# A selective-scan layer with an interleaved feed-forward network: evicting the mask and delta products from PSUM with one copy

## Chip, cores and metric

The kernel runs on one core of a Trainium2 chip. Its time is the device time in microseconds (us) of one execution. The profile is of one further execution, taken with the hardware profiler.

## What is computed

The input is x, two sequences of 1024 tokens with 512 features, 2048 tokens in all. A selective state-space layer and a feed-forward network follow each other, each with a residual and a layer norm:

```
xn    = x * rsqrt(mean(x*x) + 1e-6) * norm_w
mask  = sigmoid((xn @ select_proj_w.T + select_proj_b) * select_gate)
xn    = xn * mask
delta, B, C = split(xn @ x_proj_w.T)          # 128 columns each
delta = softplus(delta @ dt_proj_w.T + dt_proj_b)
h_t   = exp(delta_t * A) * h_{t-1} + (delta_t * xn_t) * B_t   # A = -exp(A_log), state 512 x 128
y_t   = h_t . C_t
x     = layernorm(x + (y + x * D) @ out_proj_w.T)
x     = layernorm(x + (silu(x @ w_gate.T) * (x @ w_up.T)) @ w_down.T)   # hidden 2048
```

All arithmetic is fp32. The change touches the two nonlinear stages ahead of the scan. The mask is a sigmoid and delta a softplus. The kernel makes both from softplus(v) = relu(v) + log(1 + exp(-|v|)). The sigmoid of z is exp(-softplus(-z)). So each stage needs the ReLU and the absolute value of the same product, taken with factors that differ from feature to feature (a bias, and for the mask a scale as well).

## The kernel before

The scan sets the frame. A main loop makes 1024 steps, k = 0 to 1023. Sixteen steps make a segment of 32 tokens (`st`), and eight make one half of the features of a segment. In a step:

- TensorE (PE) makes two matmul pairs that are interleaved: `bu` (L689), the input of step k, and `a` (L407), the decay of step k+1.
- ScalarE (ACT) turns the two halves of `a` into exp(-a) in SBUF (L414, the exps). They are written one step ahead of the scan that uses them, in a buffer of three steps. `a` has two PSUM banks.
- VectorE (DVE) adds the carried state to the first column (L708) and scans 32 tokens (L709).
- GpSimd (POOL) builds the operands `ddt` (L378) and `du` (L388) of coming steps.
- In some steps PE makes the outputs `y` of the half before (L426).

All other work is written as Python generators, and `work`, a small planner, mixes it in while the program is built. Nothing is decided on the chip: each engine runs its instructions in the order in which they were written. A generator yields "P" where it wants TensorE, "H" between pieces of matmul work that it holds TensorE for, and "E" where other engines must do something first. In the steps where the list `PARTS` gives a credit (4, 0, 3, 3, 0, 3, 3, 0 over eight steps), `work.give_back()` runs first and lets the generator that has just used TensorE go on: its eviction from PSUM then stands on ACT ahead of the exps of that step. After the exps `work.others()` lets every generator that stands at "E" go one yield further. After the scan, `work.tensor()` gives out pieces of matmul work up to the credit. All of this work shares one PSUM bank in the main loop (the tile "m" of `misc`, one buffer): the next piece of matmuls must wait until ACT or DVE has read the last one. During the start, before the loop, there are six such banks.

The generators are `pre(c)`, which prepares one lot of tokens for the scan; `post(tt)`, the output projection and first layer norm of 128 tokens; `ffn(tt)`, their feed-forward network; and `silu`, the activation of one piece of it. There are nine lots: two of 128 tokens (four segments each), then seven of 256 (eight segments each).

`pre(c)` runs through these stages, each needing the one before: squares and their sum (`ss`); the factor `rms`; the mask product `sel` in four pieces m, each evicted by L221 (ReLU into `u`) and L225 (absolute value into `dt`); `softplus` (Exp L318, Ln L320, two additions on POOL L323); an Exp (L230); the product with xn on POOL (L233); the products `xp` and `b`; the delta product `z` in two pieces of two features blocks, evicted by L273 and L274 for each block; `softplus` again; the product `u` on POOL (L278); its transposes `uT`, one for each 128 tokens (copy L290, then four DMAs L295 to DRAM `ub_d`); and `t`, the first delta of each segment (copy L313, DMA L314). The tiles into which L290 and L313 copy are one buffer, the tile "row": each copy waits until the DMAs that read the one before have landed.

`pre(0)` runs by itself before the loop. `pre(c+1)` is put in front of the planner's list when lot c begins. If it is not finished one segment before its tokens are due, `work.finish` writes all that is left of it at once, between two steps, together with what the other generators have at "E":

```
if lot_of[st + 1] > c:
    work.finish(pres[c + 1])
load(st + 1)
```

For lot 2 that point lies between step 111 and step 112.

Of the kernel before, what the change touches and what calls it, by code (L numbers as in the profile page):

```python
# [10 lines left out]
AF = mybir.ActivationFunctionType  # L11
# [14 lines left out]
V_NORM, V_SELB, V_GATE, V_DTB = range(4)  # L26
# [8 lines left out]
def kernel(  # L35
# [17 lines left out]
    nc = tc.nc  # L53
# [8 lines left out]
    NM = D // P  # L62
# [40 lines left out]
    gate_b = main.tile([P, NM], FP, name="gate_b")  # L103
    neg = main.tile([P, 2, NM], FP, name="neg")
# [37 lines left out]
    def col(group, m):  # L142
        return vec[:, group, m : m + 1]
# [13 lines left out]
    def misc(name):  # L157
        return bank_pool[0].tile([P, 512], FP, tag="m", name=name)
# [5 lines left out]
    def pre(c):  # L164

        t0, n = lots[c]
# [8 lines left out]
        dt = pre_pool.tile([P, NM, TC], FP, tag="dt", name=f"dt_{c}", bufs=2)  # L175
        u = pre_pool.tile([P, NM, TC], FP, tag="u", name=f"u_{c}")
        c_sb = pre_pool.tile([P, TC], FP, tag="c_sb", name=f"c_sb_{c}", bufs=2)
        rms, low, c_sb = rms[:, 0:n], low[:, 0:n], c_sb[:, 0:n]
        xT, dt, u = xT[:, :, 0:n], dt[:, :, 0:n], u[:, :, 0:n]
# [3 lines left out]
        def matmuls(ps, w, m, rhs):  # L183
            for k in range(NM):
                nc.tensor.matmul(  # L185
                    ps[:, 0:n], w[:, k, ts(m, P)], rhs[:, k, :],
                    start=(k == 0), stop=(k == NM - 1),
                )
                yield "H" if k + 1 < NM else "E"
# [10 lines left out]
        ps = misc(f"ss_{c}")  # L200
# [14 lines left out]
        yield "P"  # L215


        for m in range(NM):
            ps = misc(f"sel_{c}_{m}")
            yield from matmuls(ps, sel_w, m, xn)  # L220
            nc.scalar.activation(  # L221
                u[:, m, :], ps[:, 0:n], AF.Relu,
                bias=neg[:, 1, m : m + 1], scale=neg[:, 0, m : m + 1],
            )
            nc.scalar.activation(  # L225
                dt[:, m, :], ps[:, 0:n], AF.Abs, bias=gate_b[:, m : m + 1], scale=col(V_GATE, m)
            )
            yield "P" if m + 1 < NM else "E"
        yield from softplus(dt, u)
        nc.scalar.activation(dt, dt, AF.Exp, scale=-1.0)  # L230
        yield "E"
# [8 lines left out]
        for g, dst in ((0, low), (2, c_sb)):  # L240
            ps = misc(f"xp_{c}_{g}")
# [4 lines left out]
        ps = misc(f"b_{c}")  # L246
# [17 lines left out]
        for a in range(0, NM, 2):  # L264
            ps = misc(f"z_{c}_{a}")
            for m in (a, a + 1):
                nc.tensor.matmul(  # L267
                    ps[:, ts(m - a, n)], dt_w[:, ts(m, P)], low, start=True, stop=True
                )
                yield "H" if m == a else "E"  # L270
            for m in (a, a + 1):
                z = ps[:, ts(m - a, n)]
                nc.scalar.activation(u[:, m, :], z, AF.Relu, bias=col(V_DTB, m))  # L273
                nc.scalar.activation(dt[:, m, :], z, AF.Abs, bias=col(V_DTB, m))  # L274
            yield "P" if a == 0 else "E"
        yield from softplus(dt, u)
        for a in (slice(0, 2), slice(2, 4)):
            nc.gpsimd.tensor_tensor(u[:, a, :], dt[:, a, :], xn[:, a, :], ALU.mult)  # L278
# [2 lines left out]
        for j in range(n_j):  # L281
            yield "P"
            ps = misc(f"uT_{c}_{j}")
# [5 lines left out]
            t = pre_pool.tile([P, D], FP, tag="row", name=f"uT_{c}_{j}")  # L289
# [14 lines left out]
        ps = misc(f"t0_{c}")  # L304
# [7 lines left out]
        t = pre_pool.tile([P, D], FP, tag="row", name=f"t0_{c}")  # L312
# [3 lines left out]
    def softplus(a, r):  # L316

        nc.scalar.activation(a, a, AF.Exp, scale=-1.0)  # L318
        yield "E"
        nc.scalar.activation(a, a, AF.Ln, bias=ones[:, 0:1])  # L320
        yield "E"
        for m in (slice(0, 2), slice(2, 4)):
            nc.gpsimd.tensor_tensor(a[:, m, :], a[:, m, :], r[:, m, :], ALU.add)  # L323
            yield "E"
# [72 lines left out]
    def place(k):  # L397
        h, r = divmod(k, 8)
        m, pair = divmod(r, 2)
        return h, m, pair  # L400
# [247 lines left out]
    work = Work()  # L648

    def run(gen):  # L650
        for _ in gen:
            pass

    run(pre(0))
    diag(0, 2)
    diag(0, 3)
# [9 lines left out]
    for k in range(NG):  # L666
        h, m, pair = place(k)
# [5 lines left out]
        if r == 0:  # L673
            hs[h] = half_pool.tile([P, 256, S], FP, tag="h", name=f"h_{h}")
            if i == 0:
                c = lot_of[st]
                if c + 1 < NC and c not in begun:
                    begun.add(c)
                    pres[c + 1] = work.add(pre(c + 1), front=True)
                if st + 1 < NS:  # L680
# [3 lines that stand above are left out]
# [135 lines left out]
```

## Time and profile before

| What | Value |
|---|---|
| Median of 3 runs | 2833.24 us (2833.19 to 2833.54) |
| Profiled execution, its own time | 2842.96 us |
| Profiled execution, span from first to last instruction | 2841.2 us |
| PE busy | 2727.4 us (96%) |
| DVE busy | 2522.9 us (89%) |
| ACT busy | 1549.8 us (55%) |
| POOL busy | 1783.3 us (63%) |
| First scan begins | 43.22 us |
| Last scan ends | 2760.64 us |

The times in a profile are microseconds from the start of the span. In the timeline, each row has its start, its length, the engine, the source line, the operation, output and input, and in brackets the idle time ahead of it with what ended it. PEld are weight loads of TensorE, which run beside its matmuls; PE is busy by a model of where a matmul ends, so its 96% is not a peak rate. An fp32 matmul shows as two records. In the groups by form, the figures are the total busy time, the mean duration in ns, and the idle time ahead with the engine that ended it.

### The profile page before, as it was taken

The page shows a single profiled execution, that of the slowest core. Times are in us where ns is not written, and L with a number is a line of the kernel's source. Part 1 is how long each engine was busy: PE and PEld are TensorE (multiplying, and loading weights), DVE is VectorE, ACT ScalarE, POOL GpSimd, SP SyncE. Part 2 cuts the span into 40 slices and gives each one's busy share as a digit, 9 for nine tenths or more (in the row PEclk, how much of TensorE's full clock was granted, in tenths as well). Part 3 has the DMA queues.
Part 4 walks back from the last instruction along what each step waited for, and adds up shares of the span by engine and source line. Part 5 has one row for each costly group of instructions (what it writes and reads, how often), then busy time and mean ns, then how long its engine had stood idle before and what let it go on. Part 6 is the DMA issues. An engine that isn't in the chain of part 4 may idle for free.

```text
span 2841.2 us, 57463 instructions
## 1 busy us (share of the span) xinstructions
PE 2727.4 (96%) x22728; PEld 1484.1 (52%) x22728; DVE 2522.9 (89%) x2144; ACT 1549.8 (55%) x3105; POOL 1783.3 (63%) x2016
## 2 busy tenths in 40 slices
PE   7879999999999999999999999999999999999998
PEld 4324554555555554555544555555555555555558
DVE  2999898999999999999999999999999999999980
ACT  4546555555565455654656556555555554555442
POOL 4556675666667675775667667667576666657552
PEclk7999999999999999999999999999999999999999
DMA  2012222224223232233312333132331323332336
GB/s 75 16 30 66 86 77 79 87 73 134 86 62 116 86 121 64 83 96 105 123 43 84 105 104 104 57 100 93 112 101 47 113 87 109 101 105 96 107 103 208
DMA packets 112380, 258.67 MB, mean 91 GB/s; under 512 B 11568, under 2 KB 49456, under 8 KB 112112
## 3 DMA queue, kind: packets, MB, share of 16 engines
q1 hardware_dynamic: 112112, 254.99, 27.6%
q8 instruction: 181, 2.97, 0.4%
q14 instruction: 87, 0.71, 0.1%
HBM read 242.23 MB, written 12.71 MB: 90 GB/s over the span
## 4 chain that ended last, share of the span: by engine, by line
PE 75%; DVE 18%; issue 3%; ACT 2%; POOL 1%; DMA 0%; SPq 0%; DVEq 0%; POOLq 0%; ACTq 0%
PE bu L689 28%; PE gu L532 17%; DVE h L709 15%; PE y L426 13%; PE d L552 7%; PE a L407 4%; PE sel L185 2%; PE op L473 1%; PE xp L185 1%; DVE bu L708 1%; ACT a_sb L414 1%; PE b L249 1%; PE ss L202 0%; PE z L267 0%; DMA ub_d<-uT 0%
## 5 line engine op out<-in xcount | busy, mean ns | idle before, releaser
L709 DVE TENSOR_TENSOR_SCAN h<-a_sb,bu 128x1024 f32<-128x1024 f32 x1024 | 2341.2, 2287 | 159.2 <-POOL ddt L378 43.2
L414 ACT ACTIVATE a_sb<-a 128x496 f32<-128x496 f32 x2048 | 1089.0, 585 | 1142.6 <-PE a L407 1013.3
L689 PE MATMUL bu<-du,ub 32*128 32x512 f32 x4096 | 1198.0, 646 | 52.5 <-DVE h L709 28.3
L407 PE MATMUL a<-ddt,a_t 32*128 32x512 f32 x4096 | 1240.7, 646 | 2.8 <-ACT t L313 2.8
L378 POOL TENSOR_TENSOR ddt<-dt,hot 128x512 f32<-128x512 f32 x512 | 534.5, 1050 | 225.2 <-PE a L407 225.1
L532 PEld LDWEIGHTS gu<-x1T,w 128*128 128x128 f32 x4096 | 481.7, 192 | 232.8 <-issue 155.0
L388 POOL TENSOR_TENSOR du<-ub,hot 128x512 f32<-128x512 f32 x512 | 536.4, 1052 | 25.7 <-PE a L407 22.3
L532 PE MATMUL gu<-x1T,w 128*128 128x128 f32 x4096 | 537.3, 283 | 11.2 <-ACT t L313 4.5
L689 PEld LDWEIGHTS bu<-du,ub 32*128 32x128 f32 x4096 | 337.2, 184 | 375.8 <-issue 205.6
L426 PE MATMUL y<-h,cz 128*32 128x256 f32 x8192 | 524.7, 385 | 1.9 <-DVE h L709 1.3
L426 PEld LDWEIGHTS y<-h,cz 128*32 128x32 f32 x8192 | 227.7, 109 | 406.7 <-issue 271.9
L407 PEld LDWEIGHTS a<-ddt,a_t 32*128 32x128 f32 x4096 | 371.5, 184 | 19.9 <-ACT a_sb L414 9.6
L708 DVE TENSOR_TENSOR bu<-bu,cd 128x32 f32<-128x32 f32 x992 | 184.9, 186 | 83.1 <-PE a L407 80.2
L552 PE MATMUL d<-w,hid 128*128 128x256 f32 x1024 | 256.9, 393 | 1.1 <-ACT dt L274 1.1
L552 PEld LDWEIGHTS d<-w,hid 128*128 128x128 f32 x1024 | 183.5, 189 | 121.6 <-issue 92.5
L570 POOL TENSOR_SCALAR gu<-gu 128x256 f32<-128x256 f32 x128 | 108.3, 846 | 209.4 <-ACT gu L540 208.4
L578 POOL TENSOR_TENSOR hid<-gu,e 128x256 f32<-128x256 f32 x128 | 93.1, 728 | 141.7 <-ACT e L576 140.8
L440 POOL TENSOR_TENSOR yc<-yc,pick 128x512 f32<-128x512 f32 x64 | 66.7, 1042 | 168.7 <-ACT yc L439 168.7
L365 POOL TENSOR_TENSOR cd<-cd,h 128x256 f32<-128x256 f32 x124 | 106.5, 859 | 44.5 <-DVE h L709 44.5
L571 POOL TENSOR_TENSOR gu<-gu 128x256 f32<-128x256 f32 x128 | 93.4, 730 | 10.7
L540 ACT COPY gu<-gu 128x512 f32<-128x512 f32 x128 | 75.3, 588 | 33.5 <-PE gu L532 33.3
L323 POOL TENSOR_TENSOR dt<-dt,u 128x512 f32<-128x512 f32 (+1 forms) x36 | 41.3, 1151 | 68.7 <-ACT dt L320 68.7
(86 smaller groups left out, 1252.6 us busy)
## 6 DMA issues: line engine op xcount, KB each, us to landing
w<-in_wgu_s_dram SPq DMA_DIRECT2D x256, 512.0 KB, 3.8
w<-in_wd_s_dram SPq DMA_DIRECT2D x128, 512.0 KB, 4.0
cd<-dt_d SPq DMA_DIRECT2D x62, 256.0 KB, 4.0
ub<-ub_d SPq DMA_DIRECT2D x64, 128.0 KB, 2.0
ub_d<-bt SPq DMA_DIRECT2D x64, 64.0 KB, 1.8
ub_d<-uT SPq DMA_DIRECT2D x64, 64.0 KB, 1.8
zT<-in_x_q_dram SPq DMA_DIRECT2D x16, 256.0 KB, 4.0
x<-in_x_dram SPq DMA_DIRECT2D x16, 256.0 KB, 3.6
```

The lines of the kernel that those rows point to most:

```text
L365: nc.gpsimd.tensor_tensor(cd, cd, last, ALU.mult)
L378: nc.gpsimd.tensor_tensor(ddts[j][:, m, :, :], made[lot_of[st]][0][:, a + m, toks(st)].unsqueeze(1).to_broadcast([P, 16, S]), hot[:, ts(i, ...
L388: nc.gpsimd.tensor_tensor(dus[j][:, m, :, :], uv[:, a + m, :].unsqueeze(2).to_broadcast([P, 16, S]), hot.unsqueeze(1).to_broadcast([P, 16, ...
L407: nc.tensor.matmul(ps, a_t[ts(g, 32), m, :], ddts[k // 4][ts(g, 32), m % 2, :, :], start=True, stop=True,)
L414: nc.scalar.activation(a_sb[:, k % 3, ts(b, 16), 1:], ps[:, :, 1:], AF.Exp, scale=-1.0)
L426: nc.tensor.matmul(ys[st][ts(m, 32), ts(i, 256)], cz[st % 3][:, at : at + 32], hs[h][:, ts(m, 64), ts(b, 4)], start=(i == 0 and b == 0), s ...
L532: nc.tensor.matmul(ps[:, ts(2 * a + b, P)], w[:, a, k, :], x1T[:, k, :], start=(k == 0), stop=(k == NM - 1),)
L552: nc.tensor.matmul(ps[:, 0:HD], hid[:, f, :], w[:, f % 4, :], start=(f == 0), stop=(f == NF - 1),)
L570: nc.gpsimd.tensor_scalar_max(g, g, -80.0)
L689: nc.tensor.matmul(bu[:, ts(b, 16), :], prepared[st][ts(g, 32), 1, :], dus[k // 4][ts(g, 32), m % 2, :, :], start=True, stop=True,)
L708: nc.vector.tensor_tensor(first, first, left[:, at : at + 2, i, :], ALU.add)
L709: nc.vector.tensor_tensor_scan(hs[h][:, ts(r, 32), :].rearrange("p q t -> p (q t)"), a_sb[:, k % 3, :, :].rearrange("p q t -> p (q t)"), b ...
```

## The change

The mask stage now evicts each piece of `sel` by one plain copy into `dt`. ReLU and absolute value read `dt` from SBUF, and the absolute value is written in place. For lots 1 to 8 they are written by a generator of their own, `mask`, which stands at "E" and so comes behind the exps. For lot 0 they are written after all four copies. The delta stage evicts each pair of feature blocks by one copy. ReLU and absolute value of all four blocks follow after both copies, with two yields more than before, that is, over two visits of the planner.

```diff
+        masked = []
+        def mask():
+            for m in range(NM):
+                while m not in masked:
+                    yield "E"
+                v = dt[:, m, :]
+                nc.scalar.activation(
+                    u[:, m, :], v, AF.Relu, bias=neg[:, 1, m : m + 1], scale=neg[:, 0, m : m + 1]
+                )
+                nc.scalar.activation(v, v, AF.Abs, bias=gate_b[:, m : m + 1], scale=col(V_GATE, m))
+                if m + 1 < NM:
+                    yield "E"
+            masked.append("all")
+        if c:
+            work.add(mask(), front=True)
         for m in range(NM):
             ps = misc(f"sel_{c}_{m}")
             yield from matmuls(ps, sel_w, m, xn)
-            nc.scalar.activation(
-                u[:, m, :], ps[:, 0:n], AF.Relu,
-                bias=neg[:, 1, m : m + 1], scale=neg[:, 0, m : m + 1],
-            )
-            nc.scalar.activation(
-                dt[:, m, :], ps[:, 0:n], AF.Abs, bias=gate_b[:, m : m + 1], scale=col(V_GATE, m)
-            )
+            nc.scalar.copy(dt[:, m, :], ps[:, 0:n])
+            masked.append(m)
             yield "P" if m + 1 < NM else "E"
+        if c == 0:
+            yield from mask()
+        while "all" not in masked:
+            yield "E"
         yield from softplus(dt, u)
...
-            for m in (a, a + 1):
-                z = ps[:, ts(m - a, n)]
-                nc.scalar.activation(u[:, m, :], z, AF.Relu, bias=col(V_DTB, m))
-                nc.scalar.activation(dt[:, m, :], z, AF.Abs, bias=col(V_DTB, m))
+            nc.scalar.copy(dt[:, a : a + 2, :], ps[:, 0 : 2 * n].rearrange("p (m t) -> p m t", m=2))
             yield "P" if a == 0 else "E"
+        for m in range(NM):
+            nc.scalar.activation(u[:, m, :], dt[:, m, :], AF.Relu, bias=col(V_DTB, m))
+            nc.scalar.activation(dt[:, m, :], dt[:, m, :], AF.Abs, bias=col(V_DTB, m))
+            if m == 1:
+                yield "E"
+        yield "E"
         yield from softplus(dt, u)
```

## Prediction

> **What bounds the kernel now.** I read four things in this order: the busy shares, the groups by form, the tiles `sel` and `z` with who waited for them, and then the timeline at two places, the start and step 111. PE is 96% busy, so PE looks like the bound. The groups say more.
>
> ```profile
> L709 DVE TENSOR_TENSOR_SCAN h<-a_sb,bu 128x1024 f32<-128x1024 f32 x1024 | 2341.2, 2287 | 159.2 <-POOL ddt L378 43.2 <-PE a L407 9.0 <-PE bu L689 3.3
> L708 DVE TENSOR_TENSOR bu<-bu,cd 128x32 f32<-128x32 f32 x992 | 184.9, 186 | 83.1 <-PE a L407 80.2 <-PE bu L689 0.2
> L414 ACT ACTIVATE a_sb<-a 128x496 f32<-128x496 f32 x2048 | 1089.0, 585 | 1142.6 <-PE a L407 1013.3 <-PE bu L689 127.6
> ```
>
> A step costs DVE at least 2.287 + 0.186 = 2.47 us (the closest the scans commonly follow each other is 2.48). The real mean is (2760.64 - 2.29 - 43.22)/1023 = 2.65. So DVE and PE share the loop: most steps run at DVE's pace, and those with much other matmul work at PE's. ACT bounds neither: its exps wait 1013 us for `a`, so it has time to spare in the loop.
>
> Does the eviction that the change shortens hold anything up? These rows are from the tile `sel` (who waited for it), then from `z`:
>
> ```profile
>   PEld sel L185: 18.1, 21
>   PE sel L185: 1.3, 5
> ...
>   PEld z L267: 7.5, 8
>   PE z L267: 0.8, 2
> ```
>
> Weight loads wait 25.6 us for the bank, but the matmuls themselves only 2.1 us; while a load waits, PE still works on `bu` and `a`. From the scans' starts in the timeline, the three steps from each of the 32 L225 in the loop on are together 10.1 us above 2.48 each. That is 0.11 a step, less than the loop's mean of 0.17. The 18 steps with an L274 and the two after each give 5.3 us, 0.10 each. There is little here to win.
>
> **The change, part by part.** ACT, in the loop. Per lot of 256 tokens it adds four copies of 128x256 and two of 128x512. The nearest rows are L243 (376 ns for 128x256) and L540 (588 ns), so 7 x (4 x 0.376 + 2 x 0.588) = 18.8 us, and about 1 us for lot 1. I count these at nothing: they lie in ACT's idle time. The price if that cover were gone is those 20 us. The ReLUs and absolute values keep their sizes: 562 and 567 ns from PSUM for the mask, 482 and 487 for delta. From SBUF no such row exists with these factors; L198 has one factor and takes 503 against 482 to 487, so 0.02 each more at most, or as little as nothing. What is behind them on ACT: the next exps, for which the scan waits. In the delta stage before, four such operations took 1.6 us at one go and the scan beside them kept its pace; the new bursts are of the same four.
>
> The gain side: PE's own waits of 2.1 us are the near end, and the far end is the excess of both stages, 15.4 us, most of which is matmul time. The near end decides, since PE has `bu`, `a` and `y` to do before it takes up the bank again. I take 1 us gained.
>
> **The start.** Nothing covers it: no scan runs yet, and each stage of `pre(0)` waits for the last. Lines of ACT's timeline:
>
> ```profile
> 15.46 0.45 ACT L225 ACTIVATE dt<-sel,gate_b,vec 128x128 f32<-128x128 f32 x1
> 16.38 0.46 ACT L221 ACTIVATE u<-sel,neg 128x128 f32<-128x128 f32 x1 [0.47 <-PE sel L185]
> 16.73 0.45 ACT L225 ACTIVATE dt<-sel,gate_b,vec 128x128 f32<-128x128 f32 x1
> 17.22 0.63 ACT L318 ACTIVATE dt<-dt 128x512 f32<-128x512 f32 x1
> 17.88 0.72 ACT L320 ACTIVATE dt<-dt,ones 128x512 f32<-128x512 f32 x1
> ...
> 28.87 0.41 ACT L274 ACTIVATE dt<-z,vec 128x128 f32<-128x128 f32 x1
> 29.31 0.63 ACT L318 ACTIVATE dt<-dt 128x512 f32<-128x512 f32 x1
> ```
>
> Before, six of the eight mask operations ran while PE still made `sel`; only two stand behind the last matmul, and ACT is done at 17.19. Now the fourth copy starts at 16.38 and all eight follow it. L221 to L225 is 0.36 from start to start, since they overlap; an operation that needs the one before does not: L318 ends at 17.85 and L320 starts at 17.88. The in-place absolute value must wait for the ReLU that reads the same tile (in the built program it has a wait on ACT's own semaphore, the ReLU of the next piece has none). So a pair is 0.46 + 0.03 + 0.36 = 0.85 and four end at 16.6 + 3 x 0.85 + 0.49 + 0.45 = 20.1: 2.9 later. For delta, the second copy starts at 27.55 and is done at 27.92, and four pairs of (0.39 + 0.03 + 0.28) end at about 30.7 against 29.28: 1.5 later. Together 4.4 us. The Trainium skill (ScalarE: Activation LUTs, "What ACT_TABLE_LOAD costs") says that ACTIVATEs back to back overlap by about 93 ns; applied to all eight, the sum would be 2.4 + 1.0 = 3.4. The trace shows the overlap only where nothing is waited for, so I keep 4.4.
>
> **Step 111.** The two added yields and the later evictions move lot 2's last stages. In the order of the built programs, `uT` of lot 2 stands in steps 109 and 110 before the change, and only `t` is left for `work.finish`. After it, those steps get six `gu` matmuls each, and both `uT` and `t` fall into `finish`, behind a `gu` piece and its whole `silu`. Before:
>
> ```profile
> 333.33 1.07 PE L426 MATMUL y<-h,cz 128*32 128x256 f32 x16
> 334.47 0.59 ACT L290 COPY uT<-uT 128x512 f32<-128x512 f32 x1 [0.29 <-DMA ub_d<-uT]
> 335.11 1.05 PE L306 MATMUL t<-ident,dt 128*8 128x128 f32 x8 [0.71 <-ACT uT L290]
> 338.40 0.57 ACT L313 COPY t<-t 8x512 f32<-8x512 f32 x1 [3.34 <-DMA ub_d<-uT]
> 339.02 0.71 PE L532 MATMUL gu<-x1T,w 128*128 128x128 f32 x4 [2.87 <-ACT t L313]
> 341.60 0.20 DVE L708 TENSOR_TENSOR bu<-bu,cd 128x32 f32<-128x32 f32 x1 [5.77 <-PE a L407]
> ```
>
> The reader is to see one DMA wait: from the end of L290 (335.06) to the landing of its four DMAs is 3.34 us, ACT stands still, and PE's `gu` waits for the bank behind it. After the change the chain from the end of `y` (334.40) is: four `gu` matmuls 1.0, their copy 0.6, POOL L570 0.85, the Exp, Ln and Exp of `silu` 0.42 + 0.51 + 0.42 (with 0.1 of gaps), the first `uT` copy 0.57, so 338.9. Its DMAs land 3.34 later, 342.2. The second copy, 0.57, and its DMAs make it 346.1, where `t`'s copy stood at 338.4: 7.7 us later. All DMAs count here: eight of L295 on SP's queue, about 0.45 each to issue, and behind them `dt_d`, the loads `ub` and `cd` of segment 8 (needed five steps or more later, so hidden), and two weight loads. Nothing in DVE or PE can go on, since `bu` of step 112 stands behind on PE.
>
> The clock: after the 2.87 us of idle, matmuls `a` took 1.05 instead of 0.59 (granted clock 0.88 over 333.5 to 342). The Trainium skill (TensorE: Matmul & The Clock Gate, "What's actually happening") throttles PE after an idle window of about 3.4 us. Before already pays one slow stretch. By that rule the longer stall could double the slow part, about 1 us more; the row shows that less idle than 3.4 has sufficed, and the slow stretch ends with activity either way. So I add nothing and keep 1 us for the range.
>
> **The rest.** From step 109 to 304 fills change places, at the same count of matmuls. One visible stall goes with them: at step 147 `op` waits 2.62 us for DVE's L464 and the scan comes 3.3 us late, with `zT` one step ahead of `op`. Now `zT` is in step 142 and `op` in 144. But at steps 210 and 211 the same closeness appears, where 203 and 205 stood. Between -4 and +3, I take -1.
>
> **Sum.** +4.4 + 7.7 - 1 - 1 = +10.1 us. It is made against the profiled execution's 2842.96 us (the span of 2841.2 and 1.8 around it), so 2853. The median of the runs is 9.7 lower; as the terms are stalls of fixed length, I carry +10 over: 2843.3.
>
> **Rivals.** (1) The bank decides, and the result is faster. The place is the mask and delta stages of lots 2 to 8; the price is the weight loads' 25.6 us and some 8 us that loads of other tiles wait for L225 and L274, of which two thirds would go, as a 0.38 copy replaces 1.1 us: -22 + 12 = 2823. It decides from the point where more than half of the loads' waits are PE's idle time; 2.1 of 25.6 speaks against it. Chance 0.04. (2) `finish` costs little more, since the weights of later `gu` pieces and the matmul work done ahead in steps 109 to 111 are given back in steps 112 to 126, which have fewer fills (that is about 4 x 0.57 us of late scans in the steps of eight `gu`): +4.4 + 4 - 4, or 2837.6, no measurable change. Chance 0.10. (3) ACT's bursts come just ahead of exps in the loop: two bursts of four operations with waits are 1.9 us instead of 1.6, and ACT then needs 1.9 + 1.07 in a step of 2.48. If 1 us were lost in each of seven lots, 2850. Against it speaks that in the delta stage of before the exps end at 1181.99 and their scan starts at 1184.27, 2.3 us later. Chance 0.14. (4) That the change does not do what it says is excluded by the program's order: the bank is read once.
>
> **How the numbers follow.** My forecast, 2839 to 2848, has 0.72. A run of this kernel tells 0.2%, 5.7 us, from no change, so slower means over 2838.9. Slower is 0.72 + 0.14, the same 0.10, faster 0.04. The range takes in the second rival's edge and the third: 2837.5 to 2850.
>
> **What would show it.** The first scan at 47.6 instead of 43.2; the scan of step 112 some 16 us behind that of 111 (8.4 before) with two DMA waits on ACT; PE's waits for L225 gone and the loop's other steps unchanged. If the first scan is not later, the overlap argument is wrong; if the loop from step 310 on is shorter by over 5 us, rival 1 is right.

## The result, and the profile after

| | Before | Changed |
|---|---|---|
| Median | 2833.39 us (4 runs, 2833.19 to 2838.13) | 2861.58 us (4 runs, 2858.51 to 2864.78) |
| Profiled execution, its own time | 2842.96 | 2858.51 |
| First scan begins | 43.22 | 47.72 |
| ACT busy | 1549.8 | 1577.6 |

The changed kernel is slower: the ratio is 1.0089 (95% interval 1.0077 to 1.0101), about 25 us (28 between the two medians), where 10 were forecast. Runs of one kernel here scatter by several us from one chip and execution to the next, so each ratio below is against the runs of the kernel before that were made beside it.

The groups of the changed kernel by form show that the loop's own operations cost what they did:

```profile
L728 DVE TENSOR_TENSOR_SCAN h<-a_sb,bu 128x1024 f32<-128x1024 f32 x1024 | 2341.0, 2287 | 163.9 <-PE bu L708 51.0 <-PE a L426 9.4 <-DVE bu L727 1.4
L727 DVE TENSOR_TENSOR bu<-bu,cd 128x32 f32<-128x32 f32 x992 | 184.8, 186 | 95.4 <-PE a L426 91.1 <-PE bu L708 1.3
L433 ACT ACTIVATE a_sb<-a 128x496 f32<-128x496 f32 x2048 | 1087.8, 584 | 1120.3 <-PE a L426 989.1 <-PE bu L708 129.8
```

Only DVE's waits have grown. The change did free the bank. From the tile `sel` of the changed kernel, who waited for it:

```profile
  PEld sel L185: 9.4, 12
  PE sel L185: 0.2, 1
```

Loads waited 18.1 us before, and the matmuls themselves 1.3. Half is gone, and the time as a whole shows nothing of it.

The start, on ACT, from the changed kernel's timeline:

```profile
15.73 0.27 ACT L238 COPY dt<-sel 128x128 f32<-128x128 f32 x1 [0.63 <-PE sel L185]
15.89 0.49 ACT L225 ACTIVATE u<-dt,neg 128x128 f32<-128x128 f32 x1
16.42 0.49 ACT L228 ACTIVATE dt<-dt,gate_b,vec 128x128 f32<-128x128 f32 x1
16.82 0.48 ACT L225 ACTIVATE u<-dt,neg 128x128 f32<-128x128 f32 x1
...
19.15 0.49 ACT L228 ACTIVATE dt<-dt,gate_b,vec 128x128 f32<-128x128 f32 x1
19.68 0.63 ACT L337 ACTIVATE dt<-dt 128x512 f32<-128x512 f32 x1
```

All eight operations stand behind the last copy. The absolute value starts 0.53 after its ReLU, the next ReLU 0.40 after that. The last `sel` matmul ended at 15.70, so the Exp stands 3.98 behind it, where before it was 17.22 - 16.34 = 0.88.

Step 111, chosen rows of the same timeline:

```profile
338.91 1.16 PE L551 MATMUL gu<-x1T,w 128*128 128x128 f32 x8
340.11 0.58 ACT L559 COPY gu<-gu 128x512 f32<-128x512 f32 x1 [1.43 <-PE gu L551]
341.58 0.85 POOL L589 TENSOR_SCALAR gu<-gu 128x256 f32<-128x256 f32 x1
342.46 0.42 ACT L592 ACTIVATE e<-gu 128x256 f32<-128x256 f32 x1 [1.77 <-POOL gu L589]
343.77 0.57 ACT L309 COPY uT<-uT 128x512 f32<-128x512 f32 x1
347.56 0.58 ACT L309 COPY uT<-uT 128x512 f32<-128x512 f32 x1 [3.22 <-DMA ub_d<-uT]
351.36 0.57 ACT L332 COPY t<-t 8x512 f32<-8x512 f32 x1 [3.21 <-DMA ub_d<-uT]
353.14 1.22 PE L708 MATMUL bu<-du,ub 32*128 32x512 f32 x1
355.38 0.20 DVE L727 TENSOR_TENSOR bu<-bu,cd 128x32 f32<-128x32 f32 x1 [15.13 <-PE a L426]
```

Two DMA waits on ACT instead of one, behind a whole `silu`, and DVE idle for 15.13 us instead of 5.77. Step 111 (from scan to scan) lasts 17.73 us, before 8.36.

### The profile page after: what moved, and what is told of

Same layout as the page of the kernel before. It is cut to its first block, busy times and chain, and to the rows that moved or that the text cites. A ratio compares the mean times of both kernels' runs of the same rounds, so it can differ in the third digit from the quotient of the medians.

```text
span 2856.7 us, 57516 instructions
## 1 busy us (share of the span) xinstructions
PE 2726.7 (95%) x22728; PEld 1483.5 (52%) x22728; DVE 2523.2 (88%) x2144; ACT 1577.6 (55%) x3159; POOL 1780.5 (62%) x2016
## 4 chain that ended last, share of the span: by engine, by line
PE 74%; DVE 17%; issue 3%; ACT 3%; POOL 1%; DMA 1%; SPq 0%; DVEq 0%; ACTq 0%; POOLq 0%
PE bu L708 28%; PE gu L551 17%; DVE h L728 15%; PE y L445 12%; PE d L571 7%; PE a L426 4%; PE sel L185 2%; PE op L492 1%; ACT a_sb L433 1%; PE xp L185 1%; DVE bu L727 1%; DMA ub_d<-uT 1%; PE b L265 1%; SPq L314 0%; PE z L283 0%
## 5 line engine op out<-in xcount | busy, mean ns | idle before, releaser
L708 PE MATMUL bu<-du,ub 32*128 32x512 f32 x4096 | 1197.4, 646 | 54.5 <-DVE h L728 28.3
L551 PE MATMUL gu<-x1T,w 128*128 128x128 f32 x4096 | 536.3, 283 | 15.5 <-ACT x1T L539 7.2
L708 PEld LDWEIGHTS bu<-du,ub 32*128 32x128 f32 x4096 | 337.3, 184 | 378.2 <-issue 212.4
L727 DVE TENSOR_TENSOR bu<-bu,cd 128x32 f32<-128x32 f32 x992 | 184.8, 186 | 95.4 <-PE a L426 91.1
L589 POOL TENSOR_SCALAR gu<-gu 128x256 f32<-128x256 f32 x128 | 108.1, 844 | 225.1 <-ACT gu L559 224.2
```

The costliest lines, as they stand in the source:

```text
L551: nc.tensor.matmul(ps[:, ts(2 * a + b, P)], w[:, a, k, :], x1T[:, k, :], start=(k == 0), stop=(k == NM - 1),)
L589: nc.gpsimd.tensor_scalar_max(g, g, -80.0)
L708: nc.tensor.matmul(bu[:, ts(b, 16), :], prepared[st][ts(g, 32), 1, :], dus[k // 4][ts(g, 32), m % 2, :, :], start=True, stop=True,)
L727: nc.vector.tensor_tensor(first, first, left[:, at : at + 2, i, :], ALU.add)
```

## The experiments

The table divides each profiled execution at the starts of its scans; "Rest" runs from the last scan's start to the end of the span. All figures are us; the last column is the execution's own time, 1.8 us longer than the span. The sections below refer to it.

| Kernel | First scan | Steps 0-15 | 16-110 | 111 | 112-127 | 128-447 | 448-1022 | Rest | Time |
|---|---|---|---|---|---|---|---|---|---|
| before | 43.2 | 44.2 | 246.2 | 8.4 | 44.0 | 853.9 | 1518.6 | 82.8 | 2843.0 |
| before_again | 42.4 | 39.3 | 246.6 | 8.6 | 43.8 | 851.5 | 1518.3 | 81.2 | 2833.4 |
| changed | 47.7 | 44.6 | 245.6 | 17.7 | 42.4 | 859.0 | 1518.7 | 81.0 | 2858.5 |
| after_again | 46.6 | 44.4 | 247.7 | 17.7 | 43.0 | 860.3 | 1518.3 | 84.1 | 2863.8 |
| mask_only | 46.1 | 40.9 | 246.1 | 9.2 | 43.2 | 853.8 | 1519.5 | 80.9 | 2841.5 |
| before_yields | 43.2 | 45.7 | 244.5 | 17.2 | 43.8 | 856.5 | 1519.0 | 81.1 | 2852.8 |
| start_old | 43.0 | 40.8 | 247.4 | 17.7 | 42.5 | 858.8 | 1518.2 | 81.2 | 2851.3 |
| yields_row2 | 42.1 | 44.4 | 247.2 | 14.0 | 43.3 | 849.8 | 1516.6 | 81.9 | 2841.1 |
| before_row2 | 42.2 | 44.5 | 246.7 | 5.1 | 43.1 | 855.3 | 1517.0 | 82.1 | 2837.9 |
| after_row2 | 45.6 | 39.3 | 248.6 | 14.0 | 42.6 | 854.5 | 1519.4 | 81.2 | 2847.0 |
| loop_no_yields | 43.0 | 42.4 | 253.0 | 8.5 | 44.3 | 871.0 | 1529.6 | 81.2 | 2874.8 |
| before_delay | 47.9 | 39.1 | 246.1 | 8.4 | 44.0 | 853.8 | 1518.7 | 82.8 | 2842.6 |
| relu_first | 45.5 | 44.8 | 245.6 | 17.7 | 42.5 | 858.9 | 1518.3 | 81.2 | 2856.3 |
| mask_loop_row2 | 41.6 | 44.4 | 248.0 | 5.1 | 43.1 | 851.6 | 1516.1 | 82.0 | 2833.7 |
| before_warm | 42.4 | 39.3 | 246.7 | 8.6 | 43.8 | 851.3 | 1518.4 | 81.2 | 2833.4 |

**The kernel before once more.**

> The kernel before, unchanged, for a second profile of it. Its first profiled execution took 2842.96 us while three runs took 2833.2 to 2833.5. Theory A (the profiled execution of before was slow by chance): this one lies nearer to 2833 and is short of some of the stalls of the first, such as the late scan of step 147. Theory B (profiling itself costs 10 us): again about 2843, with the same stalls.

2833.8 us (12 runs); ratio 0.9998 (0.9989 to 1.0006). This profiled execution took 2833.43 us, so theory A holds: profiling does not cost 10 us, and the first profile of before showed a slow execution. It was slower in steps 0 to 15 (4.9 us) and around step 147 (2.5 us, which is what steps 128 to 447 differ by). The first 16 steps follow TensorE's clock, which was at half from 39.6 to 70.4 us in the first profile of before and from 30.7 to 54.6 in this one. The windows from 55 to 70 us, in this profile and then in the changed kernel's (columns: length, busy PE, PEld, DVE, ACT, POOL, granted clock, DMA share, GB/s):

```profile
55.00:70.00 15.00, 13.13 (x97) 5.91 (x95) 14.99 (x7) 9.98 (x22) 11.52 (x12) 1.00 0.01 2
```

```profile
55.00:70.00 15.00, 15.00 (x50) 8.05 (x48) 10.87 (x6) 7.33 (x17) 8.39 (x9) 0.50 0.00 1
```

At full clock DVE is busy all the time; at half clock PE is the bound, and DVE loses 4.1 us in this window alone.

**One part at a time.** mask_only has the mask part of the change, with the delta stage of before (as a diff against the changed kernel):

```diff
-            nc.scalar.copy(dt[:, a : a + 2, :], ps[:, 0 : 2 * n].rearrange("p (m t) -> p m t", m=2))
+            for m in (a, a + 1):
+                z = ps[:, ts(m - a, n)]
+                nc.scalar.activation(u[:, m, :], z, AF.Relu, bias=col(V_DTB, m))
+                nc.scalar.activation(dt[:, m, :], z, AF.Abs, bias=col(V_DTB, m))
             yield "P" if a == 0 else "E"
-        for m in range(NM):
-            nc.scalar.activation(u[:, m, :], dt[:, m, :], AF.Relu, bias=col(V_DTB, m))
-            nc.scalar.activation(dt[:, m, :], dt[:, m, :], AF.Abs, bias=col(V_DTB, m))
-            if m == 1:
-                yield "E"
-        yield "E"
```

> The change in the mask stage alone; the delta stage is that of before. The order on TensorE is that of before in every step. Theory 1 (the loss is the start, the added yields of the delta stage, and little else): only the mask's part of the start is lost, 2.9 us, so 2836. Theory 2 (added copies and waiting bursts on ACT delay the loop): 8 to 15 us lost, spread over the mask stages of lots 2 to 8. Theory 3 (the freed bank pays): 2830 or less.

2842.6 us (15 runs); ratio 1.0022 (1.0014 to 1.0029), 6 us. The order on TensorE is that of before. From the last `sel` matmul to the Exp it is 3.98 us as in the changed kernel (0.88 before), so the start loses 3.1. Some 3 us more are lost than theory 1 has. In the trace, step 86 is 1.35 us longer than in before_again, step 160 1.20 and step 153 0.40. mask_loop_row2 has the same three to 0.02 us, and neither profile of before has them. Ahead of step 86, in before and then here (its scan starts at 266.89 and at 265.05):

```profile
265.15 0.59 ACT L520 COPY x1T<-x1T 128x512 f32<-128x512 f32 x1
265.79 2.05 PE L532 MATMUL gu<-x1T,w 128*128 128x128 f32 x16 [0.29 <-ACT x1T L520]
```

```profile
262.50 0.60 ACT L225 ACTIVATE u<-dt,neg 128x256 f32<-128x256 f32 x1
263.13 0.60 ACT L228 ACTIVATE dt<-dt,gate_b,vec 128x256 f32<-128x256 f32 x1
263.76 1.06 ACT L334 ACTIVATE dt<-dt 128x1024 f32<-128x1024 f32 x1
264.73 0.57 ACT L536 COPY x1T<-x1T 128x512 f32<-128x512 f32 x1
265.35 2.05 PE L548 MATMUL gu<-x1T,w 128*128 128x128 f32 x16 [1.56 <-ACT x1T L536]
```

The last pair of the mask has moved behind the exps, and the softplus with it. They push back ACT's copy of `x1T`, the input of the feed-forward network, for which sixteen `gu` records wait. Where the next matmuls had waited for the bank, steps did get shorter (step 406: 2.98 us before, 2.55 here), but by less. So theory 1 is 3 us short, theory 2 is right in kind and too high in size, and theory 3 falls.

before_yields has nothing of the change but its two yields:

```diff
             yield "P" if a == 0 else "E"
+        yield "E"
+        yield "E"
         yield from softplus(dt, u)
```

> The kernel before with two more yields "E" ahead of the delta stage's softplus and nothing else: ACT's operations are those of before, the order on TensorE is that of the changed kernel. Theory 1: the start is as before, step 111 lasts some 16 to 18 us, and 10 to 20 us are lost, 2843 to 2853. Theory 2: the yields cost only step 111 or less, up to 9 us, since ACT has not a single operation more.

2849.2 us (4 runs); ratio 1.0044 (1.0027 to 1.0061), 13 us, with not one operation more on ACT. Step 111 takes 17.2 us, and steps 128 to 447 take 5 us more than in before_again. (Of these, 1.6 are step 211, 4.96 us here and 3.31 in yields_row2 and the first changed profile; its length differs between executions of one kernel.) Theory 1 holds, and theory 2 is too low.

start_old is the changed kernel with lot 0 evicted as before. The mask stage against the changed kernel's (the delta stage is split by `if c:` in the same way):

```diff
-            nc.scalar.copy(dt[:, m, :], ps[:, 0:n])
-            masked.append(m)
+            if c:
+                nc.scalar.copy(dt[:, m, :], ps[:, 0:n])
+                masked.append(m)
+            else:
+                nc.scalar.activation(
+                    u[:, m, :], ps[:, 0:n], AF.Relu,
+                    bias=neg[:, 1, m : m + 1], scale=neg[:, 0, m : m + 1],
+                )
...
-        if c == 0:
-            yield from mask()
-        while "all" not in masked:
+        while c and "all" not in masked:
             yield "E"
```

> The changed kernel with lot 0, which is prepared before the loop, evicted as before. Theory 1: the first scan is back at 43.2 us and the time falls by 4.5 us against the changed kernel, to about 2857. Rival: the start's loss had been made up later (a scan that starts later waits less for its operands in the first steps), so that less than 2 us come back.

2851.3 us (4 runs); ratio 1.0058 (1.0043 to 1.0073). The first scan is back at 43.0. From the changed kernel's 1.0089 to 1.0058 is some 9 us, more than the 4.7 of the start; steps 0 to 15 took 3.8 us less in this execution. From step 112 on it loses what before_yields loses and 2 us more (steps 128 to 447: 858.8 and 856.5). Step by step, six are longer than in before_yields (86 by 1.34 us, 157 by 1.12, 281 by 0.70, 298 by 0.81, 429 by 1.05, 560 by 1.50), and all five traces of kernels with both parts of the change and its two yields agree on the first five to 0.02 us. In all but step 281, PE waits for the copy of `x1T`. Others are shorter by 0.3 to 0.7, where the bank came free sooner (683: 2.99 and 2.48). From the waits of before_yields, then of the changed kernel:

```profile
PE gu L534 <- ACT x1T L522: 2.4, 2, 2.1
PE gu L551 <- ACT x1T L539: 7.2, 6, 2.1
```

So the copies and bursts of four on ACT are not free. By the two ratios, 1.0044 and 1.0058, whose intervals overlap, they cost some 4 us; by the two traces from step 16 on, 3.5.

**Without the yields.** loop_no_yields is start_old with both added yields taken out, so that all eight ReLUs and absolute values of the delta stage go at one visit.

```diff
-            if m == 1:
-                yield "E"
-        yield "E"
         yield from softplus(dt, u)
```

> The changed kernel with lot 0 evicted as before and without the two added yields: the order on TensorE is that of before in every step, and what is left of the change is the copies, ReLUs and absolute values of lots 1 to 8 on ACT. Theory 1 (start and yields are the loss): within 3 us of the kernel before, 2834 to 2837. Theory 2 (the waiting bursts delay the exps, all eight operations of the delta stage now at one go): 5 us or more slower.

2873.0 us (4 runs); ratio 1.0120 (1.0095 to 1.0145), 36 us, the slowest of all, though TensorE's order is that of before. Theory 1 falls for this kernel. Around one delta stage (two of its eight operations shown):

```profile
1204.61 0.49 ACT L302 ACTIVATE u<-dt,vec 128x256 f32<-128x256 f32 x1
1205.14 0.51 ACT L303 ACTIVATE dt<-dt,vec 128x256 f32<-128x256 f32 x1
1205.68 1.06 ACT L346 ACTIVATE dt<-dt 128x1024 f32<-128x1024 f32 x1
1206.64 1.04 ACT L442 ACTIVATE a_sb<-a 128x496 f32<-128x496 f32 x2
1207.26 0.69 PE L435 MATMUL a<-ddt,a_t 32*128 32x512 f32 x1 [1.65 <-ACT a_sb L442]
1208.46 0.20 DVE L736 TENSOR_TENSOR bu<-bu,cd 128x32 f32<-128x32 f32 x1 [1.66 <-PE bu L717]
1209.24 3.62 PE L560 MATMUL gu<-x1T,w 128*128 128x128 f32 x16 [0.39 <-ACT x1T L548]
1214.03 0.20 DVE L736 TENSOR_TENSOR bu<-bu,cd 128x32 f32<-128x32 f32 x1 [2.98 <-PE a L435]
```

Eight operations and the Exp L346 keep ACT from the exps; PE waits 1.65 us for a bank of `a`, and `bu` behind it is late. In the same stretch PE's sixteen `gu` records take 3.62 us where the next group takes 2.05: one half-clock window follows the stall. So the yields have a use: they split the burst. They lose because of where they push the later stages.

**The DMA waits.** yields_row2 is before_yields with two buffers for the tile `row`:

```diff
-            t = pre_pool.tile([P, D], FP, tag="row", name=f"uT_{c}_{j}")
+            t = pre_pool.tile([P, D], FP, tag="row", name=f"uT_{c}_{j}", bufs=2)
...
-        t = pre_pool.tile([P, D], FP, tag="row", name=f"t0_{c}")
+        t = pre_pool.tile([P, D], FP, tag="row", name=f"t0_{c}", bufs=2)
```

> The kernel before with the two yields, and with two buffers instead of one for the tile row, so that a copy no longer waits for the DMAs of the copy just ahead. Theory 1 (the yields cost through the copies that wait for DMAs, in work.finish and at the second uT copy of later lots): step 111 falls from 16 to 18 us to some 10, and the time from 2849 to about 2838 to 2841. Rival (the yields cost through the order of fills and the clock): less than 4 us come back.

2840.9 us (12 runs); ratio 1.0001 (0.9988 to 1.0013): it is as fast as the kernel before, though not as fast as that kernel with the same two buffers (before_row2 below). ACT's waits for DMA, from the waits of the changed kernel:

```profile
ACT t L332 <- DMA ub_d<-uT: 13.4, 7, 3.2
ACT uT L309 <- DMA ub_d<-uT: 7.8, 4, 3.2
```

That is 21.2 us, in before_yields 16.2, in before_again 11.1, and with two buffers none. Where they hurt is seen at step 438, of the changed kernel:

```profile
1225.52 0.58 ACT L309 COPY uT<-uT 128x512 f32<-128x512 f32 x1
1229.87 0.59 ACT L309 COPY uT<-uT 128x512 f32<-128x512 f32 x1 [2.75 <-DMA ub_d<-uT]
1230.36 1.07 ACT L433 ACTIVATE a_sb<-a 128x496 f32<-128x496 f32 x2
1230.51 1.05 PE L325 MATMUL t<-ident,dt 128*8 128x128 f32 x8 [2.22 <-ACT uT L309]
1232.73 0.20 DVE L727 TENSOR_TENSOR bu<-bu,cd 128x32 f32<-128x32 f32 x1 [1.56 <-PE a L426]
```

The written order here is that of before. But the delta stage's softplus comes two visits later, the first copy falls later in its step, and the DMAs of that copy no longer land in time for the second. Step 438 takes 4.15 us, before 2.51; with two buffers it takes 2.49. Step 189 is the other such place (3.61 us, before 2.69, with two buffers 2.48). Step 111 falls less than expected, to 14.0: the `silu` ahead of the copies stays.

after_row2 has the same two lines in the changed kernel.

> The changed kernel with two buffers for the tile row. Theory 1 (the losses of step 111 and of steps 128 to 447 come from copies that wait for the DMAs of the copy just ahead): step 111 falls from 17.7 to about 11 us, the later loss of 6 us nearly goes, and the time from 2861 to 2846 to 2851; what is left is the start and the clock. Rival (order of fills, bursts on ACT): under 5 us come back.

2846.9 us (8 runs); ratio 1.0031 (1.0020 to 1.0042), 16 us less than the changed kernel. In the trace 3.7 of them are step 111 and 4.5 steps 128 to 447; 5.3 are steps 0 to 15, which the buffers do not touch.

before_row2 has them in the kernel before.

> The kernel before with two buffers for the tile row. Theory 1: in the start the copy of t no longer waits 3.3 us for the DMAs of uT, and step 111 loses 3 of its 8.4 us: 2826 to 2830. Rival: the start is bound by the load of ub behind the same DMAs, so only step 111 gains, 2830 to 2831.

2828.8 us (17 runs); ratio 0.9968 (0.9953 to 0.9982), the fastest kernel here, ahead of both. Its runs lie at two levels, eight from 2822.5 to 2824.1 with a mean granted clock of 0.991 or 0.992, seven from 2837.0 to 2838.0 with 0.985, and the profile is of the upper one. Step 111 takes 5.1 us. The first scan stays at 42.2, as the rival said: `t`'s copy was not what the start waited for.

Since the kernel before gains 9 us by them as well, the two buffers give back less of the change than the last two ratios seem to say. With two buffers on both sides the yields still cost some 9 us (0.9968 to 1.0001) and the whole change some 18 (0.9968 to 1.0031), each to about 5 us. Step 111 takes 14.0 us in both and 5.1 without the change, though ACT waits for no DMA of `uT` in any of the three. What is left there is the `silu` ahead of the copies and matmuls at half clock behind it (those of `t` took 1.88 us in after_row2, 1.05 in before_row2). As far as these intervals tell, the DMA waits are the smaller part of the loss.

mask_loop_row2 adds the mask part of the change to it, for all lots but the first. The new lines that differ from those of the change:

```diff
-        if c == 0:
-            yield from mask()
-        while "all" not in masked:
+        while c and "all" not in masked:
             yield "E"
```

> The kernel before with two buffers for the tile row, and with the mask part of the change for lots 1 to 8 alone (the delta stage and lot 0 as before). Theory 1 (the freed bank brings nothing, since TensorE did not wait for it): within 2 us of the kernel before with two buffers, whose runs were 2822.5 to 2838. Theory 3 (it pays once the other losses are away): 3 us or more below 2822.

2832.7 us (14 runs); ratio 0.9982 (0.9974 to 0.9990), 4 us less gain than the two buffers bring alone. Steps 86, 153 and 160 are 2.9 us longer, as in mask_only. The freed bank brings no net gain here either; theory 3 falls.

**The start and the clock.** relu_first writes lot 0's ReLUs ahead of its absolute values in the changed kernel; in the delta stage (the mask stage has the like):

```diff
-        for m in range(NM):
+        for m in range(NM) if c == 0 else ():
+            nc.scalar.activation(u[:, m, :], dt[:, m, :], AF.Relu, bias=col(V_DTB, m))
+        for m in range(NM) if c == 0 else ():
+            nc.scalar.activation(dt[:, m, :], dt[:, m, :], AF.Abs, bias=col(V_DTB, m))
+        for m in range(NM) if c else ():
             nc.scalar.activation(u[:, m, :], dt[:, m, :], AF.Relu, bias=col(V_DTB, m))
```

> The changed kernel with lot 0's four ReLUs ahead of its four absolute values in both stages, so that no operation waits for the one just ahead. Theory 1 (the pairs wait for each other, as forecast): starts follow each other by about 0.39 and 0.29 instead of 0.46 and 0.36 on average, and the first scan comes 0.9 to 1.2 us earlier than the changed kernel's. Rival (the overlap is lost on operands in SBUF in any case): the first scan stays at 47.7.

2853.6 us (4 runs); ratio 1.0059 (1.0041 to 1.0077). The first scan comes at 45.5. The first stage's eight operations now run without gaps:

```profile
14.97 1.65 ACT L223 ACTIVATE u<-dt,neg 128x128 f32<-128x128 f32 x4
16.52 1.64 ACT L229 ACTIVATE dt<-dt,gate_b,vec 128x128 f32<-128x128 f32 x4
```

Each stage is 0.57 us shorter from its last matmul to its Exp, 1.14 together, as expected; the other 1.1 us of the first scan are matmuls of the start that ran at full clock in this execution.

before_warm and before_delay ask how far the clock depends on the start. before_warm adds idle matmuls to it, three behind each of the two stages and one behind `t`'s:

```diff
+        def warm(name, n):
+            ps = misc(f"warm_{name}")
+            for _ in range(n):
+                nc.tensor.matmul(ps, ident, sel_w[:, 0, :], start=True, stop=True)
...
+        if c == 0:
+            warm("sel", 3)
         yield from softplus(dt, u)
```

> The kernel before with seven idle matmuls of 128x512 on TensorE in the gaps of the start (after sel, z and t of lot 0), whose result is not used. Theory C (how long TensorE stays at half clock after the start is what differs between executions and costs the changed kernel about 5 us in its first 16 steps): the clock is full by the first steps, the scan of step 16 comes 4 to 8 us earlier, 2826 to 2829. Rival: the first steps are bound by POOL and DMA, and the clock matters little: within 1 us.

2840.1 us (12 runs); ratio 1.0011 (0.9999 to 1.0022), inconclusive in time, and its trace agrees with before_again's to 0.2 us in each column: the idle matmuls did not move the clock, and the theory was not tested by them.

before_delay makes the start longer by idle copies on ACT, in lot 0's delta stage:

```diff
+        for _ in range(7 if c == 0 else 0):
+            nc.scalar.activation(u, u, AF.Copy)
         yield from softplus(dt, u)
```

> The kernel before with seven idle copies of u onto itself on ACT in the start, ahead of lot 0's second softplus: 7 x 0.66 = 4.6 us. It has the length that the change adds to the start, and none of its operations. Theory D (only the length counts, one for one): 4.6 us slower than before, 2838 to 2840. Theory C (a later start also keeps TensorE at half clock longer into the loop): 8 to 11 us slower, with the scan of step 16 8 us or more late.

2843.5 us (16 runs); ratio 1.0022 (1.0015 to 1.0030), 6 us, which lies between the two forecasts. The first scan is 5.5 us later than in before_again, and steps 0 to 15 take 39.1. So in this execution theory D held: a longer start alone did not keep the clock low.

after_again is the changed kernel once more.

> The changed kernel, unchanged, for a second profile. In its first profile steps 0 to 15 took 44.6 us, in that of before 39.3 or 44.2, by how long TensorE stayed at half clock. Theory C (the later start of the change keeps TensorE at half clock longer): 44 to 46 us again. Theory D (that length is a matter of chance in each execution): 39.3 us is as likely, and the execution is then 5 us shorter, about 2853 to 2857. Step 111 and steps 128 to 447 take 17.7 and 859 us in either case.

2859.7 us (4 runs); ratio 1.0070 (1.0053 to 1.0087). Steps 0 to 15 took 44.4, as in the first profile. The profiles do not tell whether the changed start makes the half-clock stretch long: before, before_yields, yields_row2, before_row2 and mask_loop_row2 had 44 us or more with lot 0 evicted as before, and after_row2, with the changed start, had 39.3. The mean granted clock of each run tells more. It was 0.983 to 0.986 in all eight runs of the changed kernel and 0.987 or 0.988 in the four of start_old. In the runs of before, times near 2833.4 us go with 0.990 and times near 2842 with 0.986. The difference goes with the 4 us by which the changed kernel loses to start_old beyond its longer start. Why its clock is lower is left open.

## Why the prediction was right or wrong

The direction was right, and so were the start and the order of work in step 111; the size was not. The forecast of 2843.3 us missed the median by 18.3. Between the two first profiles, on which the sum was made, the change cost 15.5 us where the sum had 10.1. The other 12.8 lie between profiles and medians (the point on the median, below). Against before_again, whose profiled execution stands at the median of before, the changed kernel's profile is 25.1 us longer: start 5.3, steps 0 to 15 5.3, step 111 9.1, steps 128 to 447 7.5, all else -2.1.

- *Little to win from the bank*: right. PE's waits fell as the change meant and single steps got shorter, by 0.3 to 0.7 us, but neither mask_only nor mask_loop_row2 gained.
- *ACT in the loop at nothing*: this step failed. I considered only the exps behind the new operations, and not ACT's copy of `x1T`, for which `gu` waits. These waits are 7.2 us in the changed kernel and 2.4 in before_yields, and the cost is some 4 us where the prediction had nothing. ACT's idle time covers the rest, but not bursts of eight: with them the kernel lost 36 us (loop_no_yields). The operations from SBUF were dearer than my bound of 0.02 us: 600 ns at the median for the mask against 562 and 567.
- *The start, 4.4*: 3.10 + 1.60 = 4.7 by the distance from last matmul to Exp. Most of it is that all eight operations stand behind the last copy; the in-place wait makes 1.14 of it, as relu_first shows. Without that wait 3.6 are left, near the 3.4 that the prediction gave for operations that all overlap. So keeping 4.4 was right, and for the reason given.
- *Step 111, 7.7*: 9.4 between the first profiles, 9.1 against before_again. The chain came as written: the copy of `t` was forecast 11.7 us after the end of `y` and stood 351.36 - 338.98 = 12.4 after it. I had started the `gu` records at the end of `y`, which is about where they were, but POOL took up L589 0.9 us after the copy it waited for. From `t`'s copy to DVE's L727 (L708 before) it was 4.02 us instead of 3.20, more of it at half clock. That the second DMA wait decides is not shown: with two buffers on both sides step 111 still grows by 8.9.
- *The clock, nothing added*: wrong. After the stall the clock was at half for 10.2 us, in before for 3.4. Together with the chain this makes step 111 larger than forecast. Nor did the slow stretch at the start end with activity: PE was busy without a break from 43 to 70 us, at half clock.
- *The rest, -1*: the step of the sum that failed most. I considered only fills that change places, and took the same written order for the same time. The stall of step 147 went as forecast (5.81 us in the first profile of before, 2.48 after), yet steps 128 to 447 lost 5.1 (first profile of before) to 7.5 us (second). Of the 7.5, some 3.7 are the work on ACT above (steps 157, 281, 298 and 429, against before_yields), and 2.5 are steps 189 and 438, copies that wait for the DMAs of the copy just ahead once two more visits move the first copy within its step. Another 1.6 are step 398, which is chance: after_again has it as in before. The other steps, the fills that change places among them, nearly cancel, as forecast. The row of the waits in before (9 us on ACT for these DMAs) named the second hazard, and I did not use it.
- *The sum carried to the median*: this failed too, and it is the largest part of the miss. I took the stalls to be of fixed length, the same in profile and median. The first profile of before stood 9.7 us above its median, with slow first steps and the slow step 147, and this should have been explained before a sum was made against it. The first profile of the changed kernel stood 3.1 below its own. The changed kernel did not have the fast first steps in either profile, and its granted clock was 0.986 or less in all eight runs (the longer slow stretch of step 111 makes 0.001 of it), so its median did not fall below its profile as that of before did. The cause of that clock stays open.
- *Rivals*: the third, that ACT's bursts delay the exps, has its mechanism shown only for bursts of eight; bursts of four delay another copy. The second, that `finish` gives its cost back, fell: steps 112 to 127 gave back 1.3 us (1.6 against the first profile).

## What to carry to other kernels

A yield in a planned schedule is not free because it holds no work: it moves every later stage, and what it does to forced points (`finish`) and to single buffers that a DMA still reads must be followed in the written order and in time. Before a long eviction is split into a copy and work behind it, ask whether the matmul engine itself waits for the bank or only its weight loads; here the matmuls themselves waited 2 us and the loads 25. When work is moved back on an engine, look at everything that stands behind it there, not only at the next exps: here it was a copy for the feed-forward network. Before a remedy is credited with a loss, give it to the kernel before as well: the two buffers gained 9 us there. Take a second profile of the kernel before, and explain its distance to the median, before small stalls are summed against it.

## What the runs showed of the hardware

TensorE stayed at half clock for 41 us in the changed kernel (34.9 to 75.9), although its matmuls filled every microsecond from 43 to 70; in before_again it was 23.9 us. Two executions of the kernel before (30.8 and 23.9 us at half clock) differed by 5 us in their first 16 steps, which follow the clock. Later, single windows of 3.4 us at half clock stood behind short idle times: in before_again PE was idle for 1.25 and 1.33 us (to 126.7 and 129.3), and the clock was at half from 129.7 to 133.1.
